# Two extra matmuls of the identity with each state's sum, in a four-layer selective-scan kernel

## The chip, the cores and the metric

The kernel runs on one core of a Trainium2 chip. The metric is the time of one execution on the device, in microseconds. The core has TensorE (matmul; its weight loads are listed apart, as PEld), VectorE (DVE), ScalarE (ACT), GpSimd (POOL) and SyncE, which issues the transfers.

## The reference, cut to what matters

Four layers, each `x = x + SS2D(groupnorm(x))`, on x of 8 images of 48 x 48 pixels with 96 channels. In a layer, 192 inner channels go through a 3 x 3 depthwise convolution and silu, and are then scanned along the pixels in four orders (rows, columns, and both backwards), with 16 states per channel:

```python
def step(h, inp):
    u, dl, Bv, Cv = inp
    dA = jnp.exp(dl[..., None] * A)
    h = h * dA + (dl * u)[..., None] * Bv[:, :, None, :]
    y = jnp.einsum('bkdn,bkn->bkd', h, Cv)      # sum over the 16 states n
    return (h, y)
h0 = jnp.zeros((B, K, Din, N), jnp.float32)
_, ys = jax.lax.scan(step, h0, (u_t, d_t, B_t, C_t))
ys = jnp.moveaxis(ys, 0, -1)
ys = ys + xs * Ds.reshape(K, Din)[None, :, :, None]
# ... the four orders are added up, normalized over channels, gated and projected back
```

Layers 0, 1 and 2 scan so. Layer 3 computes the same sums with cumulative sums, and the kernel handles it in a shorter way.

## The kernel before

Images are taken in pairs, four pairs per layer. The 192 channels of two images lie in three tiles of 128 partitions (t = 0, 1, 2). For each pair there are 12 groups (three tiles, two directions of the image, two ways), each cut in three chunks of 768 pixels (`SCAN`), and each chunk has 16 states. One state of one chunk is a unit of work. For each:

```python
def exp(self, n, da):                     # ScalarE: dA = exp(dl * A_n)
    self.da[n] = da = da[:, : self.m]
    nc.scalar.activation(da, self.dl, AF.Exp, scale=columns_of(...))

def spread(self, n):
    # ... (layer 3's part left out)
    if self.pooled(n):                    # every fourth state: B comes by a transfer, GpSimd weighs it
        self.exp(n, pb.tile([P, 2 * BANK], F32, name="b", tag="b"))
        return
    k, w = picked(self.t, n)              # others: TensorE spreads B over 128 partitions (bf16 parts)
    self.b[n] = b = pb.tile([P, 2 * BANK], F32, name="b", tag="b")
    for z, zm in pieces(self.m):          # 768 columns: 512 and 256
        nc.tensor.matmul(
            b[:, z : z + zm], w, self.brow[:k, z : z + zm], start=True, stop=True
        )

def scan(self, n):
    # ...
    if not self.pooled(n):
        nc.vector.tensor_mul(b, self.du, b)
    if self.l < NLAYER - 1:
        h = b if self.pooled(n) else da
        nc.vector.tensor_tensor_scan(way(h), way(da), way(b), start, ALU.mult, ALU.add)
    # ...
    if not self.last:
        end = m - 1 if self.d == 0 else 0
        nc.scalar.copy(carries[:, n : n + 1], h[:, end : end + 1])
    nc.gpsimd.tensor_mul(c, c, h)         # times C, on GpSimd

def add_up(self, n):                      # TensorE sums the states into one accumulator
    if n == 0:
        self.acc = pacc.tile([P, 2 * BANK], F32, name="acc", tag="acc")
    c = self.cb.pop(n)
    for z, zm in pieces(self.m):
        nc.tensor.matmul(
            self.acc[:, z : z + zm], ident, c[:, z : z + zm],
            start=(n == 0), stop=(n == NS - 1),
        )
    if n == NS - 1:
        self.collect()                    # VectorE reads acc[:, :768] into y
```

The accumulator has 1024 columns (two banks of 512), of which 768 are used. There is one accumulator (`pacc`, one buffer), two buffers for `b` in PSUM (`pb`), nine for `cb`, five for `da`. The order in which the engines get their work is that of this loop (cut):

```python
LAG = 4
for k, ((l, p, unit), c, n) in enumerate(todo):
    # ... from two thirds of a pair on, the next pair's prologue (convolutions, projections)
    # is interleaved ("ahead"); in the first part, the last pair's epilogue ("behind")
    get_ready(k + 1)                      # loads ahead, spread(k + 1), exp two ahead
    c.scan(n)
    step(coming)                          # the next chunk's dl and du
    # ...
    if k >= LAG:
        (bl, bp, _), b, n = todo[k - LAG]
        b.add_up(n)                       # the sum of the state four back
```

So TensorE's queue holds, in this order, the spread of state k + 1, the sum of state k - 4, the spread of state k + 2, and so on. Layer 3 has a class of its own (`Edge`) with its own `add_up`.

Of the kernel before, what the change touches and what calls it, by code (L numbers as in the profile page):

```python
# [42 lines left out]
P = 128  # L43
# [3 lines left out]
NS = 16  # L47
# [17 lines left out]
SCAN = 16 * W  # L65
# [30 lines left out]
def ss2d_layers_kernel(ctx: ExitStack, tc: tile.TileContext, x_in, consts, weights, out):  # L96
    nc = tc.nc
# [25 lines left out]
    ident = cst[:, 0:P]  # L123
# [364 lines left out]
    def pieces(m):  # L488

        return [(z, min(BANK, m - z)) for z in range(0, m, BANK)]  # L490
# [11 lines left out]
    class Chunk:  # L502
# [118 lines left out]
        def add_up(self, n):  # L621
# [5 lines that stand above are left out]
                    self.acc[:, z : z + zm], ident, c[:, z : z + zm],  # L627
                    start=(n == 0), stop=(n == NS - 1),
                )
            if n == NS - 1:  # L630
                self.collect()

        def collect(self):
# [445 lines left out]
```

## Time and profile before

| | before |
|---|---|
| time, median of three runs | 25932.03 us (25880.63 to 25971.3) |
| span of the profiled execution | 25950.1 us |
| TensorE matmul busy | 20502.7 us, 79% |
| VectorE busy | 19436.9 us, 75% |
| GpSimd busy | 18407.7 us, 71% |
| ScalarE busy | 13651.9 us, 53% |
| mean granted clock of TensorE | 0.855 |
| read from HBM and written to it | 3650.53 MB, 164.07 MB |

In a line of the page's groups stand the line of the kernel, the engine, the operation, what is written and read with its shape, how often, then the busy time in us and the mean duration of one in ns, and behind the bar the engine's idle time just before these instructions, with what ended most of it. A line of the list of waits has the engine and what it wanted to run, an arrow to what it waited for, and then the total in us, how many times, and the longest. In the windows, each stage has its bounds, its length, the busy us of PE, PEld, DVE, ACT and POOL with instruction counts, the granted clock of TensorE as a share of full speed, the DMA share and GB/s. [...]

### The profile page before, as it was taken

To read this page: it belongs to the slowest core of one execution; us is meant where nothing else is said; L and a number is where in the kernel's file an instruction comes from. 1 tells how busy PE (TensorE), PEld (TensorE's weight loads), DVE (VectorE), ACT (ScalarE), POOL (GpSimd) and SP (SyncE) were. 2 spreads that over 40 slices of the span, in tenths; PEclk is the share of its full clock that TensorE was granted. 3 is DMA by queue.
4 is the path that set the end of the run, shared out by engine and by line. 5 is a ranking of instruction groups with operands and counts; after the bars stand their busy time and mean duration, and the time that the engine had idled before them with its cause. 6 is when DMAs were issued, how large, how long until landed. Compare 5 with 4: busy or idle time off the path is not lost. (4 is left out here: it accounts for less than half of the span.)

```text
span 25950.1 us, 229568 instructions
## 1 busy us (share of the span) xinstructions
PE 20502.7 (79%) x61890; PEld 9651.0 (37%) x61890; DVE 19436.9 (75%) x17126; ACT 13651.9 (53%) x23819; POOL 18407.7 (71%) x11561
## 2 busy tenths in 40 slices
PE   7787887887887887887887887887887887886886
PEld 2333333333433333333333433433433433334555
DVE  5867877876877877877877877877877877876443
ACT  4454554554554554554554554554554554555665
POOL 5767867867877867877877877877877877875332
PEclk8888888887888988898888897898898898897876
DMA  3545545545555555555555555545555555554121
GB/s 115 162 138 155 176 139 154 174 142 148 176 147 154 177 145 153 174 150 153 174 146 152 176 148 150 175 143 153 177 147 152 175 148 152 175 151 111 56 63 49
DMA packets 1714313, 3830.25 MB, mean 148 GB/s; under 512 B 224112, under 2 KB 588016, under 8 KB 1699824
## 3 DMA queue, kind: packets, MB, share of 16 engines
q1 hardware_dynamic: 1713008, 3815.46, 49.5%
q8 instruction: 500, 8.19, 0.1%
q14 instruction: 805, 6.59, 0.1%
HBM read 3650.53 MB, written 164.07 MB: 147 GB/s over the span
## 5 line engine op out<-in xcount | busy, mean ns | idle before, releaser
L626 PE MATMUL acc<-cb,cst 128*128 128x512 f32 (+1 forms) x27648 | 12436.5, 582 | 2350.2 <-POOL cb L619 1995.9
L619 POOL TENSOR_TENSOR cb<-cb,da 128x768 f32<-128x768 f32 x5184 | 9348.1, 1812 | 3056.7 <-DVE da L607 984.5
L626 PEld LDWEIGHTS acc<-cb,cst 128*128 128x128 f32 x27648 | 5543.0, 220 | 7898.7 <-issue 4396.8
L574 ACT ACTIVATE da<-dl,a 128x768 f32<-128x768 f32 x5184 | 4828.0, 933 | 5735.9 <-POOL cb L619 5703.7
L603 DVE TENSOR_TENSOR b<-du,b 128x768 f32<-128x768 f32 x5184 | 4871.6, 952 | 2871.6 <-PE b L591 2855.7
L607 DVE TENSOR_TENSOR_SCAN da<-da,carry,b 128x768 f32<-128x768 f32 x3456 | 6173.1, 1803 | 61.3 <-ACT da L574 3.5
L591 PE MATMUL b<-brow,pick 48*128 48x512 bf16 (+3 forms) x10368 | 2904.3, 366 | 2249.7 <-DVE da L607 1594.6
L546 POOL TENSOR_TENSOR bb<-bb,du 128x768 f32<-128x768 f32 x1728 | 3133.8, 1814 | 664.8 <-DMA bb<-xd 385.0
L619 POOL TENSOR_TENSOR cb<-cb,bb 128x768 f32<-128x768 f32 x1728 | 3135.8, 1815 | 594.8 <-issue 197.3
L607 DVE TENSOR_TENSOR_SCAN da<-da,b 128x768 f32<-128x768 f32 x1728 | 2983.4, 1743 | 28.4 <-ACT da L574 1.0
L607 DVE TENSOR_TENSOR_SCAN bb<-b,carry,bb 128x768 f32<-128x768 f32 x1152 | 2073.8, 1800 | 770.5 <-POOL bb L546 609.1
L591 PEld LDWEIGHTS <-pick 48*128 48x128 bf16 (+1 forms) x10368 | 758.7, 100 | 5014.5 <-DVE da L607 2729.1
L574 ACT ACTIVATE b<-dl,a 128x768 f32<-128x768 f32 x1728 | 1550.4, 897 | 654.5 <-DVE da L607 553.0
L618 ACT COPY carry<-da 128x1 f32<-128x1 f32 x3456 | 638.5, 185 | 2353.3 <-DVE da L607 2299.0
L262 PE MATMUL ps<-pad,diag 128*128 128x480 f32 (+1 forms) x4320 | 1801.6, 562 | 77.6 <-ACT u L227 48.2
L467 POOL TENSOR_TENSOR lg<-lg,w 128x384 f32<-128x384 f32 (+1 forms) x912 | 892.1, 978 | 1029.4 <-ACT w L465 847.5
L470 DVE SCALAR_TENSOR_TENSOR ps<-ps,lg 128x384 f32<-128x384 f32 (+1 forms) x912 | 499.8, 548 | 1127.0 <-POOL lg L468 1088.8
L607 DVE TENSOR_TENSOR_SCAN bb<-b,bb 128x768 f32<-128x768 f32 x576 | 1002.8, 1741 | 360.2 <-POOL bb L546 241.0
L262 PEld LDWEIGHTS ps<-pad,diag 128*128 128x128 f32 x4320 | 800.7, 193 | 884.6 <-issue 674.3
L450 PE MATMUL ps<-dts,w 6*128 6x384 f32 (+5 forms) x2432 | 946.6, 560 | 60.3 <-DVE ex L852 14.5
L468 POOL TENSOR_TENSOR lg<-lg,e 128x384 f32<-128x384 f32 (+1 forms) x912 | 889.9, 976 | 46.6
L791 PE MATMUL ps<-ey,cst 128*128 128x144 f32 (+1 forms) x4096 | 815.8, 345 | 120.4 <-ACT ey L815 104.0
(124 smaller groups left out, 17609.9 us busy)
## 6 DMA issues: line engine op xcount, KB each, us to landing
cb<-xd SPq DMA_DIRECT2D x4736, 384.0 KB
cb<-xd SPq DMA_DIRECT2D x4736, 192.0 KB
bb<-xd SPq DMA_DIRECT2D x1152, 384.0 KB
bb<-xd SPq DMA_DIRECT2D x1152, 192.0 KB
yd<-y SPq DMA_DIRECT2D x48, 1152.0 KB
ey<-yd SPq DMA_DIRECT2D x256, 216.0 KB
brow<-xb SPq DMA_DIRECT2D x576, 72.0 KB
xb<-parts SPq DMA_DIRECT2D x288, 108.0 KB
```

What stands on the lines that cost most here:

```text
L262: nc.tensor.matmul(ps[:, :m], ly.diag[:, int(t == 2), j, :], pad[:, r0 + dy : r0 + dy + nr, dx : dx + W], start=(j == 0), stop=(j == 8),)
L450: nc.tensor.matmul(o[:, :m], ly.dtw[q0 : q0 + r, k, chans], dts[q0 : q0 + r, at], start=True, stop=True,)
L467: nc.gpsimd.tensor_sub(lg, lg, w1)
L468: nc.gpsimd.tensor_add(lg, lg, e)
L546: nc.gpsimd.tensor_mul(b, b, self.du)
L574: nc.scalar.activation(da, self.dl, AF.Exp, scale=columns_of(self.l, self.t, self.ph, self.d, n))
L591: nc.tensor.matmul(b[:, z : z + zm], w, self.brow[:k, z : z + zm], start=True, stop=True)
L603: nc.vector.tensor_mul(b, self.du, b)
L607: nc.vector.tensor_tensor_scan(way(h), way(da), way(b), start, ALU.mult, ALU.add)
L619: nc.gpsimd.tensor_mul(c, c, h)
L626: nc.tensor.matmul(self.acc[:, z : z + zm], ident, c[:, z : z + zm], start=(n == 0), stop=(n == NS - 1),)
L791: nc.tensor.matmul(o, mean_w[:, cols], z[:, b, :], start=True, stop=False)
```

## The change

With each state's sum but the last of a chunk, two more matmuls are issued: the 128 x 128 identity by itself, into columns 768 to 895 of the accumulator, which nothing reads. They follow the state's own sum in TensorE's queue. They are meant to give TensorE more work of a kind that waits for nothing[...]; the result stays the same.

```diff
@@ -627,7 +627,14 @@
                     self.acc[:, z : z + zm], ident, c[:, z : z + zm],
                     start=(n == 0), stop=(n == NS - 1),
                 )
-            if n == NS - 1:
+            if n < NS - 1:
+
+                for _ in range(2):
+                    nc.tensor.matmul(
+                        self.acc[:, SCAN : SCAN + P], ident, ident, start=False, stop=False,
+                        skip_group_check=True,
+                    )
+            else:
                 self.collect()
```

## The prediction

> **What bounds the kernel now.** I read the page first: shares of busy time, the clock row of the slices, the costliest groups. Then the list of waits, the stages within one pair of images, slices as long as the clock's own step, and the timeline of TensorE.
>
> From the page's busy time, its slices and its groups:
>
> ```profile
> PE 20502.7 (79%) x61890; PEld 9651.0 (37%) x61890; DVE 19436.9 (75%) x17126; ACT 13651.9 (53%) x23819; POOL 18407.7 (71%) x11561
> PEclk8888888887888988898888897898898898897876
> L626 PE MATMUL acc<-cb,cst 128*128 128x512 f32 (+1 forms) x27648 | 12436.5, 582 | 2350.2 <-POOL cb L619 1995.9
> L619 POOL TENSOR_TENSOR cb<-cb,da 128x768 f32<-128x768 f32 x5184 | 9348.1, 1812 | 3056.7 <-DVE da L607 984.5
> L603 DVE TENSOR_TENSOR b<-du,b 128x768 f32<-128x768 f32 x5184 | 4871.6, 952 | 2871.6 <-PE b L591 2855.7
> L607 DVE TENSOR_TENSOR_SCAN da<-da,carry,b 128x768 f32<-128x768 f32 x3456 | 6173.1, 1803 | 61.3 <-ACT da L574 3.5
> ```
>
> No engine is full. L626 has 27648 records; a state's sum is two fp32 matmuls of two records each, so there are 27648 / 4 = 6912 states. They run from 274.5 us (first L607 scan) to 23711 us (last L626 start): 3.39 us per state. VectorE needs 952 + 1803 = 2.76 us for three states of four, and one scan of 1.74 to 1.80 us for the fourth: some 2.5 us. The rest is idle time, and TensorE is what VectorE waits for most (the list of waits):
>
> ```profile
> DVE b L603 <- PE b L591: 2855.7, 1796, 18.3
> PE acc L626 <- POOL cb L619: 1995.9, 1329, 7.1
> PE b L591 <- DVE da L607: 1594.6, 1325, 4.5
> ```
>
> TensorE runs in program order: the sum of a state four back (L626, waiting for GpSimd's product), then the spread of B for a coming state (L591, waiting for a buffer that a scan frees). Whatever holds up the sum holds up the spread, and so VectorE. The granted clock makes it worse, at 0.855 in the mean. One pair of images, cut at its stages (columns: stage, us, busy us per engine, then clock, DMA share, GB/s):
>
> ```profile
> 8178.00:9348.00 1170.00, 956.16 (x2979) 445.20 (x2980) 1025.39 (x870) 644.36 (x1144) 953.95 (x581) 0.88 0.55 174
> 9348.00:9742.00 394.00, 339.56 (x937) 153.72 (x935) 257.71 (x212) 209.28 (x336) 249.94 (x161) 0.92 0.48 131
> 9742.00:10140.00 398.00, 261.98 (x611) 106.69 (x611) 255.67 (x199) 157.25 (x285) 265.17 (x177) 0.77 0.50 137
> ```
>
> The first two thirds of a pair are near VectorE's limit (1025 of 1170 us). In the next sixth the convolutions of the following pair share TensorE, which is the fullest engine (340 of 394 us, against 258 on VectorE). In the last sixth nothing is full and the clock is lowest.
>
> Slices of 3.413 us, laid on the clock's own steps, in the same columns:
>
> ```profile
> 8911.00:8914.41 3.41, 2.85 (x11) 1.12 (x9) 3.41 (x4) 3.15 (x8) 3.25 (x2) 1.00 0.85 243
> 8914.41:8917.83 3.42, 1.37 (x6) 0.30 (x4) 3.42 (x3) 1.76 (x4) 3.42 (x4) 1.00 0.47 177
> 8917.83:8921.24 3.41, 3.10 (x5) 1.85 (x6) 2.05 (x4) 1.87 (x3) 3.41 (x3) 0.50 0.00 0
> 8921.24:8924.65 3.41, 3.40 (x13) 1.69 (x12) 3.41 (x4) 2.23 (x6) 2.54 (x2) 1.00 0.35 112
> ```
>
> A slice in which TensorE was busy 1.37 us is followed by one at half clock, where VectorE falls to 2.05 us; a full slice brings the clock back. I did this for the whole trace, taking TensorE's streaming time (columns over clock) in each slice. At full clock, slices streaming under 35% are practically always followed by half clock (594 of 595), 35 to 50% in 45% of 717 cases, 50 to 70% in 15% of 1113, above 70% in 1% of 2957. At half clock the way back needs 70 to 80% (28%), 80 to 90% (62%), over 90% (87%)[...]. In all, 2206 of some 7590 slices are at half clock, in about 1115 episodes.
>
> [...] only 0.50 and 1.00 occur, in steps of 3.413 us. [...] here two sums in a row add no visible load time (below). The thresholds are from the trace[...].
>
> **The change, part by part.** Nothing is removed and nothing moved. After 15 of 16 sums two fp32 matmuls of 128 columns are added: 6912 x 15/16 = 6480 states, 12960 calls, 25920 records, since each call is two. They wait for nothing (the identity is constant, the accumulator is already held by this chunk), they come after the sum's last record, and the 16th state has none, so the read-out of the accumulator isn't held up.
>
> Size, from TensorE's timeline (start, us, records):
>
> ```profile
> 6024.56 1.56 PE L626 MATMUL acc<-cb,cst 128*128 128x512 f32 x4 [1.82 <-POOL cb L619]
> 6031.90 2.93 PE L626 MATMUL acc<-cb,cst 128*128 128x512 f32 x4 [0.39 <-POOL cb L619]
> 8833.80 2.85 PE L626 MATMUL acc<-cb,cst 128*128 128x512 f32 x8
> ```
>
> A sum takes 1.56 us, two in a row 2.85, so one streams in 1.29 us: 768 columns twice, 0.84 ns for a column. The added 2 x 128 columns twice cost 512 x 0.84 = 0.43 us at full clock, and 0.86 us at half clock (2.93 against 1.56). That is 2.8 ms of TensorE's time at full clock and 5.6 at half, hidden wherever TensorE waits anyway.
>
> *Cost.* For each wait of VectorE for a spread, I went back through the unbroken run of TensorE's work before it and counted the sums in it; each would carry 0.43 or 0.86 us more. At full clock there are 1.6 sums per wait in the first two thirds (42 waits per pair), 2.0 in the convolution stage (33 waits), 0.4 in the last sixth (24); at half clock some 0.5 (54 waits). With at most three counted per wait, that is 29 + 27 + 4 + 13 + 2 + 10 = 85 us per pair, 1.0 ms over 12 pairs. A run with two waits in it is counted twice, so I take three quarters, 0.77 ms, and add 0.12 ms for waits that are new: cost 0.9 ms.
>
> *Gain.* Each sum adds 0.43 / 3.41 = 13 points to its slice's streaming share, 25 at half clock. Moving the slices up by this times their number of sums (0.7 in a slice streaming 35 to 50%) takes the drops from 1115 to about 815. The way back becomes likelier (about 70% per slice instead of 50%), so an episode lasts 1.4 slices instead of 2.0. Half-clock slices go from 2206 to some 1150 to 1200, and the mean clock to about 0.92. VectorE's waits for spreads in half-clock slices are now 43 + 11 + 34 = 88 us per pair; with about half of the slices gone and the others rather worse I take 40 us saved, 0.48 ms. Of the 151 us of such waits per pair at full clock I put a sixth down to work left over from a slow slice: 0.3 ms. Gain 0.78 ms.
>
> Sum: 0.9 - 0.78 = 0.1 ms slower. The fourth layer, from 23.7 ms on, adds its sums elsewhere (L746) and doesn't change.
>
> **Rivals.** *The clock was the main loss.* Over the chunks of 16 states in the first two thirds, time against mean clock gives a slope of about 40 us per unit of clock on 48.5 us. A clock of 0.92 instead of 0.87 would save 2 us a chunk, or 0.6 ms there alone; with little of the cost exposed the kernel ends at 25.2 to 25.4 ms. Against it: a stall of GpSimd's causes both the low clock and the long chunk, and the extra matmuls cannot run while the sum ahead of them waits (595 slices stream under 35%). *TensorE becomes the bound.* At half clock a group of four states already needs 3 x 0.64 (the spread: 768 columns once) + 4 x 2.58 = 12.2 us of it, against 3 x 2.76 + 1.8 = 10.1 us of VectorE, and would need 4 x 0.86 more, 15.6. If the episodes stay as many, that and the convolution stage make it 26.8 ms or more. *All hidden:* the matmuls fall into idle time, the idle time that remains is GpSimd's, and nothing moves: 25.9 ms.
>
> **Range and chances.** Two terms of 0.8 to 0.9 ms stand against each other, each known to about half of itself, so their difference has a spread of some 0.6 ms. The sum is 26.0 ms; I keep 26000 us, with 25250 to 26800 for eight times in ten. More than 2% faster is below 25413 us: 0.25. More than 2% slower is above 26451 us: 0.23. Within: 0.52.
>
> **What would show it.** TensorE's records should rise by 25920, with the added group at about 0.43 us of streaming per state. The clock should be 0.90 to 0.94; a clock near 0.86 makes the gain step wrong. L603's idle before "PE b" should stay within 2400 to 3300 us, shorter in the first two thirds at half clock, longer in the convolution stage. That stage should grow from 394 us by 10 to 27 us per pair; if it doesn't, the cost step is wrong. I would be wrong altogether if [...] the loads of the identity aren't hidden at 128 columns.

## The result, and the profile after

| | before | changed kernel |
|---|---|---|
| time, median of four runs | 25939.65 us (25880.63 to 25971.3) | 26973.31 us (26941.71 to 27002.21) |
| ratio to before, 95% interval | | 1.0401 [1.0379, 1.0423] |
| TensorE matmul records | 61890 | 87810 |
| mean granted clock | 0.855 | 0.892 |
| half-clock slices of 3.413 us, episodes | 2207, 1115 | 1705, 879 |

The change makes the kernel 4.0% slower, 1.03 ms. That is outside the range of the prediction, although the clock rose. (In the traces of both kernels the granted clock is 0.50 or 1.00, and each stretch of it up to the last lasts a multiple of 3.413 us, a slice; an episode is an unbroken run of slices at half clock.) The page of the changed kernel, first its busy time and clock row, then its groups:

```profile
PE 22314.2 (83%) x87810; PEld 13034.7 (48%) x87810; DVE 19658.6 (73%) x17126; ACT 13633.1 (51%) x23806; POOL 18446.5 (68%) x11561
PEclk8898998998998998998998998998998998998886
L626 PE MATMUL acc<-cb,cst 128*128 128x512 f32 (+1 forms) x27648 | 11771.6, 549 | 1239.6 <-POOL cb L619 753.8
L619 POOL TENSOR_TENSOR cb<-cb,da 128x768 f32<-128x768 f32 x5184 | 9364.7, 1812 | 2590.5 <-DVE da L607 1110.0
L603 DVE TENSOR_TENSOR b<-du,b 128x768 f32<-128x768 f32 x5184 | 4894.5, 949 | 2041.3 <-PE b L591 2032.3
L607 DVE TENSOR_TENSOR_SCAN da<-da,carry,b 128x768 f32<-128x768 f32 x3456 | 6240.3, 1807 | 137.7 <-DVE b L603 2.7
L633 PE MATMUL acc<-cst 128*128 128x128 f32 x25920 | 4256.1, 289 | 0.0
```

The added group is the last line. The surprise is the others: the two waits that the prediction worked with are *shorter*. VectorE waits 2032 us for spreads instead of 2856, and TensorE 754 us for GpSimd's products instead of 1996. Nothing ran slower by itself either (scan 1807 ns against 1803, product 1812 both times). So the lost millisecond stands in other waits. From the list of waits of the changed kernel (engine and what it wanted to run, what it waited for, total us, times, longest):

```profile
ACT da L574 <- POOL cb L619: 7658.6, 3677, 8.5
DVE ps L470 <- POOL lg L468: 1648.1, 634, 160.6
POOL bb L546 <- DMA bb<-xd: 988.0, 531, 5.5
DVE bb L607 <- ACT b L574: 915.9, 619, 7.1
```

The same four lines of the kernel before:

```profile
ACT da L574 <- POOL cb L619: 5703.7, 3134, 9.3
DVE ps L470 <- POOL lg L468: 1088.8, 443, 161.6
POOL bb L546 <- DMA bb<-xd: 385.0, 299, 4.7
DVE bb L607 <- ACT b L574: 168.7, 147, 3.2
```

The second is a wait of VectorE for GpSimd while the next chunk's `dl` is made, 559 us longer. The last two concern the fourth states, whose B comes by a transfer (`bb`) and is weighed by GpSimd: VectorE's scan of such a state now waits 747 us longer for ScalarE's exponential, and GpSimd's weighing 603 us longer for its transfer. In none of the four lines does an added matmul wait or end the wait; whether these delay the instructions on a longer way is for the experiments. The same pair of images, cut at its stages as in the prediction, in the changed kernel:

```profile
8468.00:9709.00 1241.00, 1049.12 (x4393) 625.87 (x4394) 1039.83 (x866) 637.93 (x1136) 953.43 (x579) 0.92 0.55 163
9709.00:10121.00 412.00, 373.68 (x1324) 203.80 (x1322) 261.81 (x217) 213.65 (x343) 253.46 (x163) 0.94 0.46 129
10121.00:10509.00 388.00, 276.29 (x972) 153.25 (x972) 256.79 (x200) 157.62 (x285) 265.21 (x177) 0.85 0.52 141
```

The first two thirds of the pair grew most (1170 to 1241 us), where TensorE had room and the clock rose from 0.88 to 0.92. As means over all 12 pairs, from a stage's first scan to the next stage's, the first two thirds went from 1164.2 to 1239.7 us, the convolution stage from 389.0 to 408.7, the last sixth from 399.6 to 388.7; 12 x (75.5 + 19.7 - 10.9) = 1012 us, so this accounts for the loss of 1034.

What explains longer waits at instructions that the change doesn't touch is found in the two programs' lists of instructions. The description of the kernel before says that TensorE's queue has the order of the written loop. **That is not so.** The order of each engine's instructions is made when the program is built, and it is made anew for another program. (The trace shows it too: 842 times in the kernel before, half a sum stands alone between two spreads, and in the changed kernel 197 times.) With the added matmuls left out, these shares of the instructions stand at another place in their engine's list than before:

```
TensorE 65%   VectorE 54%   ScalarE 58%   GpSimd 50%   SyncE 49%
mean displacement, places: 2.8  1.7  2.5  1.2  1.5
```

The second row has the means over all instructions, moved or not.

On VectorE, between two scans of fourth states (B), with m the multiplication by `du` and S another scan, the kernel before most often has B m m S S m S (644 of 1728 stretches, 73 in the changed kernel). The changed one most often has B m S m S m, with or without a further S (767 stretches, 311 before), and in 647 stretches instead of 195 another scan follows B directly: there B has mostly moved ahead of the scan before it. So the one diff is two changes: more work for TensorE, and another order on all engines.

### The profile page after: what moved, and what is told of

Read it like the earlier page. It is cut to its first block, busy times and chain, and to the rows that moved or that the text cites. A ratio compares the mean times of both kernels' runs of the same rounds, so it can differ in the third digit from the quotient of the medians.

```text
span 26939.8 us, 280004 instructions
## 1 busy us (share of the span) xinstructions
PE 22314.2 (83%) x87810; PEld 13034.7 (48%) x87810; DVE 19658.6 (73%) x17126; ACT 13633.1 (51%) x23806; POOL 18446.5 (68%) x11561
## 5 line engine op out<-in xcount | busy, mean ns | idle before, releaser
L626 PE MATMUL acc<-cb,cst 128*128 128x512 f32 (+1 forms) x27648 | 11771.6, 549 | 1239.6 <-POOL cb L619 753.8
L619 POOL TENSOR_TENSOR cb<-cb,da 128x768 f32<-128x768 f32 x5184 | 9364.7, 1812 | 2590.5 <-DVE da L607 1110.0
L626 PEld LDWEIGHTS acc<-cb,cst 128*128 128x128 f32 x27648 | 5150.6, 208 | 6648.7 <-issue 5134.4
L603 DVE TENSOR_TENSOR b<-du,b 128x768 f32<-128x768 f32 x5184 | 4894.5, 949 | 2041.3 <-PE b L591 2032.3
L607 DVE TENSOR_TENSOR_SCAN da<-da,carry,b 128x768 f32<-128x768 f32 x3456 | 6240.3, 1807 | 137.7 <-DVE b L603 2.7
L591 PE MATMUL b<-brow,pick 48*128 48x512 bf16 (+3 forms) x10368 | 2801.5, 355 | 2306.6 <-DVE da L607 1236.5
L633 PEld LDWEIGHTS acc<-cst 128*128 128x128 f32 x25920 | 4239.8, 206 | 521.7 <-issue 100.0
L633 PE MATMUL acc<-cst 128*128 128x128 f32 x25920 | 4256.1, 289 | 0.0
L450 PE MATMUL ps<-dts,w 6*128 6x384 f32 (+5 forms) x2432 | 877.2, 537 | 197.4 <-DVE du L474 104.9
```

Of the source, the lines that this page charges most:

```text
L450: nc.tensor.matmul(o[:, :m], ly.dtw[q0 : q0 + r, k, chans], dts[q0 : q0 + r, at], start=True, stop=True,)
L591: nc.tensor.matmul(b[:, z : z + zm], w, self.brow[:k, z : z + zm], start=True, stop=True)
L626: nc.tensor.matmul(self.acc[:, z : z + zm], ident, c[:, z : z + zm], start=(n == 0), stop=(n == NS - 1),)
L633: nc.tensor.matmul(self.acc[:, SCAN : SCAN + P], ident, ident, start=False, stop=False, skip_group_check=True,)
```

## The experiments

All times are medians of timed runs; ratios are to the kernel before, on the same chip. Two theories at the start. WORK: the added matmuls themselves delay the spreads. ORDER: the matmuls cost little, and the new order of the other instructions costs the rest.

### The two halves apart

The program of before (or that of the change) is built first and each engine's order noted. Then the program to be run is built with every instruction tied behind its predecessor on its own engine: a tie of issue order that waits for nothing to finish. Added matmuls stand right behind their sum. The core of the edit:

```diff
+    first = build(extra=0, traced=traced)      # extra=2: the order of the changed kernel
+    issued = [i.name for b in first.main_func.blocks for i in b.instructions]
+    nc = build(order={"traced": traced, "issued": issued})
...
+        for was in order["issued"]:
+            name = now[was]                    # the same instruction in this program
+            while name is not None:            # it, and the matmuls added behind it
+                i = by_name[name]
+                if i.engine in tail:
+                    tc.add_manual_dep(i, tail[i.engine], no_sync, reason="order")
+                tail[i.engine] = name
+                name = follows.get(name)
```

No added matmuls, before's order imposed on itself (what the method costs):

> The kernel before, no extra matmuls, with the issue order of every engine written down from it and imposed on the build. A control: every theory expects the time of before, a ratio of 0.997 to 1.003 (25.85 to 26.02 ms) and a clock of 0.85 to 0.86.

Measured: 25937.85 us, ratio 0.9996 [0.9988, 1.0005]. The ties cost nothing.

Two added matmuls, all else in before's order:

> The two extra matmuls with each sum, but every engine's other instructions in the order of before. Theory ORDER (the loss comes from the other issue order that the build gave all engines): 0.98 to 1.01 of before, clock about 0.90 to 0.93, VectorE's wait for the spreads shorter. Rival WORK (the loss is the extra work of TensorE): 1.03 to 1.05, as the change itself, with VectorE's wait for the spreads grown by about 1 ms.

Measured: 26122.18 us, ratio 1.0067 [1.0050, 1.0084], clock 0.903.

No added matmuls, the changed kernel's order:

> No extra matmuls, but every engine's instructions in the order that the build gave the changed kernel. Theory ORDER: slower than before by at least as much as the change, 1.03 to 1.06 (26.7 to 27.5 ms), clock 0.86 or lower[...]. Rival WORK: 0.995 to 1.005.

Measured: 26827.43 us, ratio 1.0342 [1.0325, 1.0360], clock 0.849.

So 0.67% belongs to the matmuls and 3.42% to the order; together 4.1%, against 4.0% measured for both. The program without a single added matmul has the long waits of the changed one (its lines are numbered two higher):

```profile
DVE b L605 <- PE b L593: 1723.9, 937, 14.8
DVE ps L472 <- POOL lg L470: 1674.5, 646, 162.0
DVE bb L609 <- ACT b L576: 1050.2, 621, 7.5
```

With the matmuls but in before's order, the wait for ScalarE is back below before's 168.7 us, and the wait for spreads is a little above before's 2855.7:

```profile
DVE b L605 <- PE b L593: 3073.7, 1913, 11.7
DVE bb L609 <- ACT b L576: 118.3, 123, 2.0
```

One such stall as a timeline of the run with the changed kernel's order and no added matmul (start, us, engine and line, in brackets what it waited for):

```profile
8905.53 1.81 POOL L548 TENSOR_TENSOR bb<-bb,du 128x768 f32<-128x768 f32 x1 [1.81 <-DMA bb<-xd]
8907.30 3.59 POOL L621 TENSOR_TENSOR cb<-cb,da 128x768 f32<-128x768 f32 x2
8909.15 0.94 ACT L576 ACTIVATE da<-dl,a 128x768 f32<-128x768 f32 x1 [4.38 <-POOL cb L621]
8910.07 0.90 ACT L576 ACTIVATE b<-dl,a 128x768 f32<-128x768 f32 x1
8911.07 1.76 DVE L609 TENSOR_TENSOR_SCAN bb<-b,bb 128x768 f32<-128x768 f32 x1 [3.07 <-ACT b L576]
```

GpSimd waits 1.81 us for the transfer of a fourth state's B; its next product is late by that; ScalarE, which needs a buffer which that product frees, waits 4.38 us and then computes one exponential ahead of the one that VectorE needs; VectorE stands for 3.07 us. Three engines wait in a row, and TensorE is not among them.

### Is it one engine's order?

As above with two added matmuls, but only one engine tied to before's order and the others left to be ordered anew (the condition is shortened):

```diff
-            if was not in now:
+            if was not in now or engine_of(now[was]) not in {"PE"}:    # or DVE, Activation, Pool
                 continue
```

> The two extra matmuls; only TensorE's other instructions are held in the order of before, the build orders the other engines anew. If TensorE's order is what costs (its spreads are issued further ahead of the sums, so the sums free their buffers later): 1.00 to 1.015. If VectorE's order is what costs (a fourth state's scan pulled ahead of the scan before it, so that VectorE stands waiting for ScalarE's exponential): 1.025 to 1.05, as VectorE's order stays new.

> The two extra matmuls; only VectorE's instructions are held in the order of before. If VectorE's order is what costs: 1.00 to 1.015, and its wait for ScalarE's exponential b falls from some 900 us back to about 170. If TensorE's order costs: 1.025 to 1.05.

> The two extra matmuls; only ScalarE's instructions are held in the order of before. If the loss comes from ScalarE's exponential for the fourth state being issued behind one that waits for a buffer of GpSimd: 1.00 to 1.015. If it comes from VectorE's or TensorE's order: 1.025 to 1.05.

> The two extra matmuls; only GpSimd's instructions are held in the order of before. If GpSimd's order is the cause (it weighs B before the transfer has landed, which holds up its products and through them ScalarE): 1.005 to 1.02, and its wait for B's transfer falls from 988 us to some 400. If not: 1.03 to 1.06, as for TensorE and VectorE.

| tied to before's order | us | ratio |
|---|---|---|
| TensorE | 27466.37 | 1.0594 [1.0564, 1.0625] |
| VectorE | 27235.12 | 1.0505 [1.0473, 1.0537] |
| ScalarE | 26526.69 | 1.0232 [1.0202, 1.0262] |
| GpSimd | 27541.10 | 1.0626 [1.0608, 1.0644] |

None comes near the 1.0067 of all engines tied, and three are worse than the changed kernel with none tied. Only ScalarE's order takes something back. VectorE in before's order, for instance, waits just 266 us for ScalarE's `b`, but 2737 us for spreads. To put one engine's order back is thus not enough. How much of the loss is one engine's share these runs can't say, as the engines left free don't keep the changed kernel's order either: with TensorE tied, 48% of VectorE's instructions stand elsewhere than in the changed kernel, and with VectorE tied, 48% of ScalarE's.

That left the fourth states' scans, which the new order pulls ahead on VectorE. Without added matmuls, before's order with 885 of the 1728 such scans pulled ahead of the scan before them, and the changed kernel's order with 567 put back:

```diff
+            if pooled and at[s] < at[b] and ...:  # pull: b is the fourth state's scan, s the one before
+                moved[b], moved[s] = None, (b, s)
+            # put back: the same where at[b] < at[s], with (s, b)
```

> No extra matmuls, every engine in the order of before, but on VectorE 885 of 1728 fourth-state scans are pulled ahead of the scan before them. If that place is the cause: 1.02 to 1.05. If not: 0.995 to 1.01.

> No extra matmuls, every engine in the order of the changed kernel, but on VectorE the 567 fourth-state scans that stand ahead of the scan before them are put back behind it. If that place of the scans is the cause: 1.00 to 1.015 instead of 1.034, and VectorE's wait for ScalarE's exponential b falls from 1050 us to under 400. If the cause lies on GpSimd, ScalarE or in the transfers: 1.03 to 1.04.

Measured: pulled ahead 26869.23 us, 1.0372 [1.0355, 1.0389]; put back 27041.51 us, 1.0435 [1.0417, 1.0452]. Pulling scans ahead is *enough* to lose as much as the whole new order, though the run pulls more of them: a scan follows B directly in 1080 stretches, against 647 in the changed kernel. In the run that pulls them:

```profile
DVE b L607 <- PE b L595: 3181.8, 1944, 10.6
DVE bb L611 <- ACT b L577: 567.4, 472, 4.4
```

VectorE stands at a scan whose exponential ScalarE hasn't made yet, 567 us instead of 169, and at spreads, 3182 us instead of 2856. These are not the changed kernel's waits, which are shorter for spreads and longer for ScalarE. And putting the scans back does not repair the new order; it makes it worse. Only 80 stretches are then left in which a scan follows B directly, fewer than before, and the wait for ScalarE falls only from 1050 to 737 us. So the place of these scans isn't what makes the new order slow. An engine's order is good or bad only beside those of the others. Which part of the new orders costs what stays open: an order mixed from both programs, engine by engine, was not run.

### What the matmuls themselves cost and bring

Two added matmuls of 8 columns instead of 128, with the order left to be built (21 to 36% of each engine's instructions stand elsewhere than before):

```diff
-                        self.acc[:, SCAN : SCAN + P], ident, ident, start=False, stop=False,
+                        self.acc[:, SCAN : SCAN + 8], ident, ident[:, :8], start=False, stop=False,
```

> Two extra matmuls of 8 columns instead of 128, everything free in its order as in the change: a sixteenth of the extra streaming (about 0.03 us a state), but the build again gives another order (about a third of each engine's instructions stand elsewhere than in before). Theory ORDER: any other order may cost; 1.005 to 1.035, clock 0.85 to 0.87. Rival WORK: 0.998 to 1.004.

Measured: 26494.64 us, 1.0220 [1.0190, 1.0249], clock 0.866. This could still be order. So the same edit in before's order:

> The two extra matmuls of 8 columns with every engine held in the order of before: the counterpart of the run in which the build was free and lost 2.2%. Theory ORDER (all of that 2.2% is the order): 0.998 to 1.004. Rival (the mere presence of four more loads and matmuls per state costs): 1.01 to 1.02.

Measured: 26461.53 us, 1.0216 [1.0199, 1.0233], clock 0.870. ORDER fell here: with a sixteenth of the columns, in the same order, the added matmuls cost three times what the full ones do. And the other order of the free build cost nothing (1.0220 against 1.0216): not every new order is a worse one. In before's order, VectorE's wait for spreads, with 8 columns and then with 128:

```profile
DVE b L605 <- PE b L593: 3452.0, 2057, 12.5
DVE b L605 <- PE b L593: 3073.7, 1913, 11.7
```

TensorE's loads in the run with 8 columns, then its matmuls (start, us from the first start to the last end, records):

```profile
8803.73 0.63 PEld L636 LDWEIGHTS acc<-cst 128*128 128x128 f32 x4
8803.94 0.51 PE L636 MATMUL acc<-cst 128*128 128x8 f32 x4
8804.31 1.10 PE L628 MATMUL acc<-cb,cst 128*128 128x512 f32 x2
```

And with the full 128 columns, also in before's order:

```profile
8612.39 0.61 PE L636 MATMUL acc<-cst 128*128 128x128 f32 x4
8612.84 1.46 PE L628 MATMUL acc<-cb,cst 128*128 128x512 f32 x4
```

From the first added matmul to the next other one passes 0.37 us with 8 columns and 0.45 with 128 (medians at full clock over more than 5000 groups each: 364 and 444 ns). Each of the four records has its own load of 128 columns. By the 0.84 ns per column of a sum, 8 columns stream in some 7 ns (an estimate), and yet the records start 112 ns apart at full clock, as their loads do; at half clock it is 214 ns from load to load. So with 8 columns the spacing goes with the loads; no run with smaller loads tests whether they set it. (With 128 columns the spacing is 112 ns too, but there a record's streaming, 128 x 0.84 = 107 ns by the same estimate, is about as long.)

So the 8-column version holds TensorE for 82% of the time (364 / 444) but raises the mean clock much less (0.857 to 0.870, against 0.903). The drops to half clock do become fewer, 856 instead of the control's 1137, nearly as few as with 128 columns (789); but an episode lasts 2.4 slices instead of 1.9 (2024 slices in 856 episodes, 2174 in 1137). With such matmuls an episode ends later, not sooner.

The 8-column version's 2.2%, 0.54 ms over the 12 pairs by stage means, is thus the cost with little of the gain. If the cost goes by the time that TensorE is held, the full version has at least this cost, and its 0.67% means that the better clock gives back some 1.5 points, 0.4 ms: an estimate, as no run separates the two.

Half and twice the work, in before's order:

```diff
-                for _ in range(2):
+                for _ in range(1):             # or 4
```

> One extra matmul of 128 columns per sum, every engine in the order of before: half the dose. If [...] the added work costs later, one is the better number: 0.993 to 1.000, clock 0.88. If cost and gain both grow with the number, half of the two's loss: 1.002 to 1.005.

> Four extra matmuls per sum, every engine in the order of before: double the dose, 0.86 us more streaming per state at full clock. The clock has little left to gain (0.93 or so), so the added work shows: 1.02 to 1.05, with VectorE's wait for the spreads at 1.5 times that of the two. If the work lies in idle time, 1.01 or less.

Measured: one 26022.13 us, 1.0046 [1.0029, 1.0063], clock 0.880; four 27098.77 us, 1.0461 [1.0444, 1.0479], clock 0.935. From two to four the clock still rises (0.903 to 0.935) and the time jumps: VectorE's wait for spreads, from the lists of waits, is 2977.5 us with one, 3073.7 with two, 4279.4 with four. At four TensorE shows 89% busy on the page, the fullest engine by far (VectorE 72%).

### Where they would do no harm

Behind a sum, the added matmuls stand ahead of the next spread or sum. Ahead of a sum they can run while that sum waits for GpSimd's product. In before's order, two ahead of each sum but the chunk's first:

```diff
+            for _ in range(2 if n > 0 else 0):
+                nc.tensor.matmul(self.acc[:, SCAN : SCAN + P], ident, ident,
+                                 start=False, stop=False, skip_group_check=True)
             for z, zm in pieces(self.m):
                 nc.tensor.matmul(self.acc[:, z : z + zm], ident, c[:, z : z + zm], ...)
```

> The two extra matmuls ahead of each sum (but a chunk's first) instead of behind it, every engine in the order of before: where the sum waits for GpSimd's product, they run in that wait. If the place decides, 0.99 to 1.002 with the clock at 0.90 or more; if only the amount counts, as behind the sum, 1.004 to 1.009.

Measured: 25763.47 us, 0.9949 [0.9932, 0.9965], clock 0.916. The same, with none in the two groups (t == 2, ph == 0) during which the next pair's convolutions share TensorE:

```diff
-            for _ in range(2 if n > 0 else 0):
+            for _ in range(2 if n > 0 and not (self.t == 2 and self.ph == 0) else 0):
```

> As the two ahead of the sum in the order of before, but none in the two groups during which the next pair's convolutions run. If the matmuls' remaining cost lies there (that stage is 8 us per pair longer with them): 0.989 to 0.993. If the stage only hands its time on: 0.994 to 0.997.

Measured: 25671.15 us, 0.9904 [0.9888, 0.9921], clock 0.909. This beats both kernels, by the ratios 1.0% under the kernel before and 4.8% under the changed one. Its pair of images by stage:

```profile
8058.00:9207.00 1149.00, 1029.01 (x4419) 586.64 (x4418) 1027.48 (x872) 644.44 (x1144) 953.14 (x581) 0.95 0.57 177
9207.00:9600.00 393.00, 339.00 (x940) 153.30 (x938) 257.95 (x211) 209.49 (x337) 250.55 (x161) 0.92 0.49 132
9600.00:9990.00 390.00, 271.53 (x971) 148.59 (x971) 256.08 (x199) 156.43 (x285) 265.00 (x177) 0.86 0.52 140
```

All three stages are at or below before's 1170, 394 and 398 us, and VectorE's wait for spreads over the whole run is 2522.5 us. The clock of the first stage, 0.95, is hardly more than the 0.94 with the matmuls behind the sum, where that stage of the same pair took 1163 us; so most of the difference is that less of their cost is exposed.

## Why the prediction was wrong

**The step that failed** is the one ahead of all sums: "TensorE runs in program order: the sum of a state four back ..., then the spread of B for a coming state", and with it "Nothing is removed and nothing moved". The order was taken from the written loop instead of from the program's own instruction lists. Half to two thirds of the instructions of every engine moved (49 to 65%), and that alone costs 3.42%. No rival named it; all three spoke of TensorE.

**The sum for what it did cover** came out right within its spread. With the other instructions held in before's order, the change costs 0.18 ms (26122.18 - 25937.85), where 0.9 - 0.78 = 0.1 ms was worked out. That it came so near is in part luck: both terms were too large, by the estimates below, and the errors cancelled.

- *Records and streaming.* 25920 more records, as predicted. 0.43 us per state was predicted; four spacings of 0.111 us make 0.444 us.
- *Cost, 0.9 ms.* The 8-column run lost 0.54 ms for 82% of the holding time, and a little of that was given back by a slightly better clock. Scaled by 1 / 0.82, an estimate, this is about 0.66 ms: the term was too large by about a third. The convolution stage, predicted to grow by 10 to 27 us per pair, grew by 9 with the order held (389.0 to 397.8, mean of 12 pairs) and by 20 in the changed kernel.
- *Gain, 0.78 ms.* Taking 0.66 - 0.18, it was about 0.5 ms, an estimate too. That the clock rises was right: predicted 0.90 to 0.94, measured 0.903 with the order held, and just below it, 0.892, in the changed kernel. The drops fell from 1115 to 789 (predicted 815), but half-clock slices from 2207 only to 1482, where 1150 to 1200 were predicted: an episode still lasts 1.9 slices, not 1.4. That the way back becomes likelier is the part of this step that failed: with the added matmuls the clock drops less often; it comes back hardly sooner (after 2.0 slices in the mean before, 1.9 with them).
- *L603's idle time*, predicted at 2400 to 3300 us: 3074 with the order held, 2032 in the changed kernel, where the waits went to other instructions.

**The rivals.** "The clock was the main loss" is not borne out. With the order held, the clock of the first two thirds rose from 0.87 to 0.93 and their chunks took 48.6 us instead of 48.5 (means of 12 pairs); ahead of the sums it rose to 0.94 and they took 47.8, a gain of 0.7 us where the slope of 40 us per unit of clock would give 2.9. How much of the rest the added work took back is open. The prediction's own objection, that a stall makes both the clock low and the chunk long, fits, but no run shows it alone. "TensorE becomes the bound" is wrong at two added matmuls (0.67%) and fits at four (4.6%). "All hidden" is nearly reached ahead of the sums, not behind them.

The range was built from the two terms' errors alone. It held nothing for a change of the program that isn't in the diff.

## What to carry to other kernels

Before a cost is worked out from an engine's order, read that order from the instruction lists of both programs: a diff of a few lines can move half of the instructions on engines which it doesn't touch, and here that cost five times what the lines cost. To measure the lines alone, impose the old order on the new program, all engines at once, with an empty change as control. Here, matmuls added only for the clock paid ahead of the matmul that waits (0.9949), not behind it (1.0067), and best when the stage in which TensorE is already the fullest engine was left out (0.9904).

## What the runs showed of the hardware

A matmul of 8 fp32 columns held TensorE nearly as long as one of 128 (364 against 444 ns for two calls of two records); each record has its own load of 128 columns, and at full clock the loads start 112 ns apart. The mean clock rose far less by it: to 0.870 against 0.903, with the same records, in the same order. Drops became nearly as rare (856 against 789), but an episode at half clock lasted 2.4 slices against 1.9. I had expected such matmuls to cost next to nothing, and "busy" on the page, at 86% for 8 columns and 85% for 128, to go with the granted clock; it doesn't.
